# First mixture: last rows stored from spare buffers, node numbers read as rows and turned by PE; results of both mixtures read back by SP and POOL, two mask rows by POOL

## The chip, the cores and the metric

The kernel runs on one core of a Trainium2 chip. Its time is the device time of one execution in microseconds. Three runs of the kernel before gave a median of 2898.42 us (2892.7 to 2900.67). The engines are called PE (matmul, with its weight loads as PEld), DVE (vector), ACT (scalar), POOL (GpSimd) and SP (which here only issues transfers). ACT, POOL and SP each issue DMA transfers from their own queue of instructions.

## What is computed

A graph of 2708 nodes with 256 features passes through four layers. Each layer adds a graph attention and then a second network to x:

```
x = x + gnn_i(layernorm(x), adj) ;  x = x + ffn_i(layernorm(x))      i = 0..3
ffn_0: slice attention with a scan      ffn_1: first mixture (top 1 of 8)
ffn_2: attention, then second mixture   ffn_3: one linear layer
       (top 2 of 8, SwiGLU)
ffn_1: H = gelu(x W1 + b1)                     2708 x 1024
       p = softmax(H Wg + bg);  e = argmax(p)  one of 8 experts for each node
       y = (H Wd[e] + bd[e]) * p[e]            2708 x 256
```

gnn_1 is an attention over the neighbours in four heads, gnn_2 and gnn_3 have one head.

## The kernel before, in words

All is float32. The nodes are 22 tiles of 128 rows, the last of 20; x lies in SBUF as `X`. A tiling framework keeps each engine's instructions in program order (but for those put behind a named one by `issue_after`), sets the semaphores, and hands out buffers from pools: a tile with `bufs=3` waits for what used the one three before it. A pool's tiles of one tag share the same buffers.

**First mixture** (`top1_ffn`). The first loop goes over six blocks of 512 nodes (four tiles; the last has two). For each: `hidden` (PE L911, gelu on ACT L915) makes H transposed, in two halves of four 128-wide slices; `features` normalizes and turns the next block; `gate` makes the logits; `Routing.chunk` counts each node's place among those of its expert, and POOL scatters the node's number, 4 bytes, to that place of a list in DRAM `fnodes` (L1444, a tile an instruction). `store` turns H back to rows: for each tile and half four PE transposes (L926), a copy from PSUM into `hr` (L927, on DVE for the first half and on ACT for the second), and a store of 128 x 512 numbers by SP (L930) into DRAM `hidden`. `hr` has three buffers, which `q4` of the gate shares. Blocks 0 to 3 are stored in their own turn; blocks 4 and 5, six tiles and twelve stores, only after the gate of block 5.

Then `finish` computes how the list is cut into tiles of 128 places: a first tile for each of the eight experts, and further tiles up to 26 (`usual`); what lies beyond is run under a condition (`others`). SP loads the node numbers: `load_first` those of the first eight tiles (L1554, 128 partitions with eight numbers each), `load` one further tile at a time (L1550, one number to a partition), each with a start that SP reads from a register. `numbers` (L980) casts them to integers; `places` computes where the results go. For each tile: `fetch` (L990, POOL) gathers 128 rows of `hidden`, `transposes` (L1003, copies L1004) turns them, L1035 multiplies by the expert's `wd`, L1041 adds `bd`, and `send` (L1573, POOL) scatters the results to DRAM. Numbers and places of later tiles are made in groups of four, two tiles ahead of the first gather that needs them (`s + 6 == g[0]`, where four are fetched ahead). `owners` and `weights` (with the softmax over the logits, copied at L1532) stand behind the first cast; ACT's part of the next layer's preparation is `Head`.

**Reading the results back** (`combine`, for both mixtures, one choice in the first and two in the second). Six blocks are read with 128 x 4 x 256 numbers, 512 KB, each (the last as 128 and 20 rows); the issuing engine alternates (L1594). DVE adds each tile into X with its weight (L1604). All reads are issued ahead of the adds. The next graph layer follows at once: statistics of the rows (L144, L145), a square root on ACT (L147, which needs a table load after other functions), reciprocal (L151), normalized rows (L108), PE transposes (L1134).

**Mask.** The attention loops multiply by a mask (L675 and its like) in 22 row tiles. `mark_empty` writes two rows for nodes without neighbours into its last tile (L2053, L2054, from `flags`), once ahead of the loop of the second layer (near 691 us) and once in `reload_graph`, where the mask is read again after the second mixture has used its room: a memset by POOL (L2058), 22 loads by SP (L2060) and the two rows by ACT.

In the built program the transfers of SP and ACT take eight completion semaphores in turn, and those of POOL eight others; a transfer waits for the one eight before it in that row.

Of the kernel before, what the change touches and what calls it, by code (L numbers as in the profile page):

```python
# [16 lines left out]
P = 128  # L17
# [839 lines left out]
def top1_ffn(net, ctx):  # L857
# [6 lines left out]
    with ExitStack() as inner:  # L864
# [21 lines left out]
        with tc.tile_pool(name="f1tp", bufs=2, space=PSUM) as ptp, tc.tile_pool(  # L886
            name="f1h", bufs=2, space=PSUM
        ) as ph, tc.tile_pool(name="f1g", bufs=1, space=PSUM) as pg, tc.tile_pool(
            name="f1r", bufs=2
        ) as rp, tc.tile_pool(name="f1work", bufs=2) as work:  # L890
            w1 = work.tile([P, 2, HID], F32, name="w1", bufs=1)
            nc.gpsimd.dma_start(w1, a["f1_w1"].rearrange("(c p) m -> p c m", p=P))

            def features(its):
                ft = work.tile([P, 2, 512], F32, name="ft")
                for k, t in enumerate(its):
                    r = rows(t)
                    f = rp.tile([P, D], F32, name="f", bufs=2)
                    net.normed(f, t, ln)
                    ps = net.transposed(ptp, f, r)  # L900
                    nc.vector.tensor_copy(ft[:, :, k * P : k * P + r], ps[:, :, :r])
                return ft

            def hidden(ft, nw):

                wide, bufs = (512, 3) if nw == 512 else (nw, 2)
                halves = [work.tile([P, KC // 2, wide], F32, name=f"ht{wide}", bufs=bufs) for _ in range(2)]
                for k in range(KC):
                    ps = ph.tile([P, 512], F32, name="h")
                    for c in range(2):  # L910
                        nc.tensor.matmul(  # L911
                            ps[:, :nw], w1[:, c, k * P : (k + 1) * P], ft[:, c, :nw], start=c == 0, stop=c == 1
                        )
                    part = halves[k // (KC // 2)][:, k % (KC // 2), :]
                    nc.scalar.activation(part[:, :nw], ps[:, :nw], AF.Gelu, bias=b1[:, k : k + 1])  # L915
                return halves

            def store(its, halves):

                for k, t in enumerate(its):  # L920
                    r = rows(t)
                    for n, half in enumerate(halves):
                        hr = rp.tile([P, 512], F32, name="hr", bufs=3)
                        ps = pg.tile([P, 4, P], F32, name=f"hr{n}")
                        for c in range(KC // 2):
                            nc.tensor.transpose(ps[:r, c, :], half[:, c, k * P : k * P + r], net.ident)  # L926
                        (nc.scalar.copy if n else nc.vector.tensor_copy)(  # L927
                            hr[:r], ps[:r].rearrange("p c m -> p (c m)")
                        )
                        nc.sync.dma_start(rows_of[span(t), n * 512 : (n + 1) * 512], hr[:r])  # L930

            def gate(its, halves, nw):
                ht = [half[:, k, :] for half in halves for k in range(KC // 2)]
                pq = pg.tile([P, 512], F32, name="pq")
                for c in range(KC):
                    g = c % 4 * 32
                    nc.tensor.matmul(pq[g : g + 32, :nw], wg[:, c, :], ht[c][:, :nw], start=c < 4, stop=c >= 4)
                q4 = rp.tile([P, 512], F32, name="q4", tag="hr", bufs=3)
                nc.vector.tensor_copy(q4[:, :nw], pq[:, :nw])
                pr = pg.tile([P, 4, E], F32, name="pr")  # L940
                for k, t in enumerate(its):
                    r = rows(t)
                    nc.tensor.matmul(pr[:r, k, :], q4[:, k * P : k * P + r], add4, start=True, stop=True)
                    nc.vector.tensor_tensor(route.logits[:r, t, :], pr[:r, k, :], bg[:r], ALU.add)
                for _ in route.chunk(rp, pg, its[0], len(its), None):
                    pass


            blocks, kept = chunks(512), []
            ft = features(tiles_of(*blocks[0]))  # L950
            for n, (n0, nw) in enumerate(blocks):
                its = tiles_of(n0, nw)
                halves = hidden(ft, nw)
                if n + 1 < len(blocks):
                    ft = features(tiles_of(*blocks[n + 1]))
                gate(its, halves, nw)
                kept.append((its, halves))
                if n + 2 != len(blocks):
                    for k in kept:
                        store(*k)  # L960
                    kept.clear()
        route.finish()
        prep = ctx.enter_context(tc.tile_pool(name="g2prep", bufs=1))
        with tc.tile_pool(name="f1t", bufs=1, space=PSUM) as pt, tc.tile_pool(
# [2 lines left out]
            bd = sp.tile([P, E, D], F32, name="bd", bufs=1)  # L967
            nc.scalar.dma_start(bd.rearrange("p e d -> p (e d)"), a["f1_bd"].rearrange("e d -> (e d)").partition_broadcast(P))

            node, number, to = (  # L970
                sp.tile([P, route.tiles], t, name=name, bufs=1)
                for t, name in ((F32, "node"), (I32, "number"), (I32, "to"))
            )
            usual = route.usual
            groups = [range(E)] + [range(s, min(s + 4, usual)) for s in range(E, usual, 4)]
            held = {}

            def numbers(group):
                g = slice(group[0], group[-1] + 1)
                nc.vector.tensor_copy(number[:, g], node[:, g])  # L980

            def places(group):
                g = slice(group[0], group[-1] + 1)
                at = sp.tile([P, E], F32, name="at", bufs=2)[:, : len(group)]
                nc.vector.tensor_tensor(at, node[:, g], route.taken[:, g], ALU.mult)
                nc.vector.tensor_tensor(to[:, g], at, route.spare[:, g], ALU.add)

            def fetch(s):
# [21 lines left out]
                    return slice(s, s + 1)  # L1010
                return bass.ds(engine.value_load(route.expert[0:1, s : s + 1], min_val=0, max_val=E - 1), 1)

            route.load_first(node[:, :E])
            for s in range(E, usual):
                route.load(s, node[:, s : s + 1])
            numbers(groups[0])
            for s in range(4):
                fetch(s)
            ready = transposes(0)
            route.owners()  # L1020
            places(groups[0])
            route.weights(one)
            heads = []

            def through(s0, s1, ready):
                last = added = None
                for s in range(s0, s1):
# [13 lines left out]
                    added = nc.vector.tensor_tensor(y, ps, bd[:, e, :].rearrange("p e d -> p (e d)"), ALU.add)  # L1041
                    route.send(to[:, s : s + 1], y)
                    with tc.issue_after(added.ins):
                        for g in groups[1:]:
                            if s + 6 == g[0]:
                                numbers(g)
                                places(g)
                        if s == 3:
                            heads.append(Head(net, prep, one, "g2", True, nc.scalar))
                    if s + 4 < s1:  # L1050
# [2 lines left out]
            through(0, usual, ready)  # L1053
            with route.others():
                group = range(usual, route.tiles)
                for s in group:
                    route.load(s, node[:, s : s + 1])
                numbers(group)
                places(group)
                for s in group:  # L1060
                    fetch(s)
                through(usual, route.tiles, transposes(usual))
# [259 lines left out]
class Routing:  # L1322
# [216 lines left out]
    def load(self, s, f):  # L1539

        sync = self.net.nc.sync
        if s < self.E:
            self.loaded = sync.dma_start(f, self.hs[s * CAP : s * CAP + P, :])
            return

        with nullcontext() if s == self.usual else self.net.tc.issue_after(self.loaded.ins):
            row = sync.value_load(
                self.row[0:1, s : s + 1], min_val=0, max_val=(self.E - 1) * CAP + (NT - 1) * P
            )
        self.loaded = sync.dma_start(f, self.hs[bass.ds(row, P), :])  # L1550

    def load_first(self, f):

        self.loaded = self.net.nc.sync.dma_start(  # L1554
            f, self.hs.rearrange("(e c) d -> c (e d)", e=self.E)[:P, :]
        )

    def where(self, work, s, f):
# [24 lines left out]
    def combine(self, pool):  # L1583
# [3 lines left out]
        for n, (n0, nw) in enumerate(chunks(512)):  # L1587
            its = tiles_of(n0, nw)
            ys = []
            for c in range(self.choices):  # L1590
                y = pool.tile([P, 4, D], F32, name=f"y{c}", bufs=len(chunks(512)))
                for k0, k1, r in whole_and_rest(its):
                    r0 = (c * NT + its[k0]) * P
                    (nc.sync, nc.scalar)[(n + c) % 2].dma_start(  # L1594
                        y[:r, k0:k1, :],
                        self.ys[r0 : r0 + (k1 - k0 - 1) * P + r, :].rearrange("(t p) d -> p t d", p=r),
                    )
                ys.append(y)
# [450 lines left out]
def mark_empty(net):  # L2049

    row = net.mask[SPARE : SPARE + 1, LAST, :]
    whole = LAST * P
    net.nc.scalar.dma_start(row[:, :whole], net.flags[:LAST])  # L2053
    net.nc.scalar.dma_start(row[:, whole:], net.flags[LAST:NT, : N - whole])  # L2054


def reload_graph(net, kept):
# [101 lines left out]
```

## Time and profile before

| what | value |
|---|---|
| median of three runs (lowest to highest) | 2898.42 us (2892.7 to 2900.67) |
| the profiled execution's own time | 2896.45 us |
| its span, first to last instruction | 2894.7 us |
| granted PE clock, mean over the span | 0.946 |
| PE, PEld busy | 2651.2 us (92%), 1624.4 us (56%) |
| DVE, ACT, POOL busy | 1441.4 (50%), 1041.2 (36%), 369.5 us (13%) |
| instructions | 32765 |
| DMA | 113729 packets, 197.70 MB |

The profile is one execution. "Busy" leaves out waits and the issuing of transfers. In the lists of the trace, a row in order of time has the start, the duration, the engine and the program's line, the operation with what it writes and reads, and in brackets how long the engine had been idle and what released it; `SPq`, `ACTq` and `POOLq` are the issues of transfers by these engines. A releaser is inferred: where several were awaited, the last by the records is named. The first mixture's last stores lie near 1211 to 1234 us, the read-back of the first mixture near 1366 to 1394 us, that of the second near 2577 to 2600 us.

### The profile page before, as it was taken

How to read it: one execution, taken by the hardware profiler on the slowest of the kernel's cores; microseconds unless marked ns; L12 is line 12 of the kernel's file. 1: busy time of each engine (PE TensorE's matmuls, PEld its weight loads, DVE VectorE, ACT ScalarE, POOL GpSimd, SP SyncE). 2: the span in 40 equal slices, each digit the busy share in tenths (PEclk: the TensorE clock that was granted, in tenths of full speed). 3: DMA queues.
4: the chain of work that ended last, by engine and by line, in shares of the span. 5: the costliest groups of instructions: out<-in, count | busy, mean ns of one | idle time of the engine just before them, and what ended most of it. 6: DMA issues, size and time to landing. Idle time of an engine off the chain costs nothing. (4 is left out here: it accounts for less than half of the span.)

```text
span 2894.7 us, 32765 instructions
## 1 busy us (share of the span) xinstructions
PE 2651.2 (92%) x11893; PEld 1624.4 (56%) x11893; DVE 1441.4 (50%) x3062; ACT 1041.2 (36%) x1658; POOL 369.5 (13%) x462
## 2 busy tenths in 40 slices
PE   6999989799999989878899899998979999969998
PEld 5667746563333334567688433333346677747885
DVE  7753358344777774432644455455543222235455
ACT  3344433224665643211543223233312222215453
POOL 0000012100000001133300123223321111110002
PEclk9999999698999998989999999899969999989999
DMA  8899210000000005354200100002021111041001
GB/s 298 280 292 312 104 65 1 8 1 1 1 1 1 1 19 173 91 166 130 87 1 0 34 22 17 15 0 93 15 101 41 34 30 34 28 137 59 1 1 39
DMA packets 113729, 197.70 MB, mean 68 GB/s; under 512 B 12380, under 2 KB 71636, under 8 KB 110732
## 3 DMA queue, kind: packets, MB, share of 16 engines
q1 hardware_dynamic: 92758, 147.89, 16.1%
q0 software_dynamic: 13120, 38.06, 4.0%
q10 hardware_dynamic: 7690, 9.62, 1.1%
q8 instruction: 99, 1.62, 0.2%
q14 instruction: 62, 0.51, 0.1%
HBM read 135.82 MB, written 59.71 MB: 68 GB/s over the span
## 5 line engine op out<-in xcount | busy, mean ns | idle before, releaser
L675 DVE SCALAR_TENSOR_TENSOR e<-e,mask 128x768 f32<-128x768 f32 (+2 forms) x264 | 411.7, 1574 | 310.9 <-ACT e L674 310.7
L674 ACT ACTIVATE e<-big_p,minus_one,ratio 128x768 f32<-128x768 f32 (+2 forms) x264 | 394.9, 1513 | 363.4 <-PE acc L1236 229.8
L1236 PE MATMUL acc<-V,e 128*128 128x257 f32 (+1 forms) x1936 | 433.5, 383 | 4.5 <-DVE e L675 4.4
L1236 PEld LDWEIGHTS acc<-V,e 128*128 128x128 f32 (+1 forms) x1936 | 352.3, 186 | 85.7 <-issue 32.1
L780 PE MATMUL acc<-e,V 128*64 128x512 f32 (+1 forms) x1056 | 249.7, 550 | 4.1 <-DVE e L675 4.1
L1878 PE MATMUL h<-w,ft 128*128 (+1 forms) x752 | 233.0, 452 | 0.5 <-ACT ft L1860 0.5
L284 PE MATMUL acc<-F,e 128*128 128x257 f32 x968 | 226.3, 384 | 3.3 <-DVE e L281 2.9
L284 PEld LDWEIGHTS acc<-F,e 128*128 128x128 f32 x968 | 173.4, 185 | 67.3 <-DVE e L281 28.7
L780 PEld LDWEIGHTS acc<-e,V 128*64 128x64 f32 x1056 | 95.4, 137 | 180.6 <-issue 159.0
L1719 PE MATMUL sc<-qt,kt 64*128 64x512 f32 (+4 forms) x656 | 187.0, 535 | 4.1 <-ACT e L1729 2.4
L1729 ACT ACTIVATE e<-sc 128x1024 f32<-128x1024 f32 (+4 forms) x140 | 102.8, 760 | 204.5 <-PE sc L1719 188.4
L1878 PEld LDWEIGHTS h<-w,ft 128*128 128x128 f32 x752 | 136.0, 191 | 56.7 <-issue 1.4
L281 DVE TENSOR_TENSOR e<-e,mask 128x512 f32<-128x512 f32 (+2 forms) x132 | 80.4, 625 | 149.4 <-ACT e L275 147.8
L1737 DVE TENSOR_TENSOR sum<-sum,e 128x1024 f32<-128x1024 f32 (+4 forms) x102 | 103.8, 1018 | 99.1 <-ACT e L1729 97.4
L275 ACT ACTIVATE e<-score 128x512 f32<-128x512 f32 (+2 forms) x132 | 69.7, 544 | 179.2 <-PE score L273 153.0
L1734 PE MATMUL po<-e,V 128*64 128x512 f32 (+5 forms) x560 | 119.4, 511 | 14.8 <-ACT e L1729 8.8
L1910 PE MATMUL po<-w,ht 114*128 (+1 forms) x564 | 129.5, 379 | 0.9 <-DVE ht L1903 0.9
L1719 PEld LDWEIGHTS sc<-qt,kt 64*128 64x128 f32 x656 | 71.8, 198 | 94.8 <-issue 80.9
L788 PE MATMUL den<-e,low 128*3 128x512 f32 (+1 forms) x1056 | 123.1, 542 | 0.0
L1910 PEld LDWEIGHTS po<-w,ht 114*128 114x128 f32 x564 | 106.7, 189 | 22.6 <-DVE ht L1903 8.2
L1563 DVE TENSOR_SCALAR second<-f,down 128x1 f32<-128x1 f32 x47 | 10.0, 213 | 213.6 <-DMA f<-hs 213.6
L273 PE MATMUL score<-QK 128*128 128x512 f32 (+2 forms) x264 | 112.1, 554 | 1.2 <-ACT e L275 0.7
(605 smaller groups left out, 3501.0 us busy)
## 6 DMA issues: line engine op xcount, KB each, us to landing
row<-in_adj SPq DMA_DIRECT2D x21, 1354.0 KB
raw<-in_adjT SPq DMA_DIRECT2D x35, 768.0 KB
hs<-zero SPq DMA_DIRECT2D x8, 2838.0 KB
hidden<-hr SPq DMA_DIRECT2D x42, 256.0 KB
wd<-in_f_wd SPq DMA_DIRECT2D x8, 1024.0 KB
kept<-mask SPq DMA_DIRECT2D x21, 338.5 KB
mask<-kept SPq DMA_DIRECT2D x21, 338.5 KB
f<-hs SPq DMA_DIRECT2D x47, 129.0 KB
```

The source lines that it names most:

```text
L273: nc.tensor.matmul(ps[:r, :iw], QK[:, 0, span(j)], QK[:, 1, i0 : i0 + iw], start=True, stop=True)
L284: nc.tensor.matmul(acc[k][:ri], e[:r, k * P : k * P + ri], F[:r, j, :], start=j == 0, stop=j == NT - 1)
L674: nc.scalar.activation(v, big_p[:, i], AF.Relu, bias=net.minus_one, scale=ratio)
L675: return nc.vector.scalar_tensor_tensor(v, v, 1.0, net.mask[:, j, i], ALU.add, ALU.mult)
L780: nc.tensor.matmul(acc[n][half, :iw], V[:, j, h, :], e[:, k, i0 : i0 + iw], start=j == 0, stop=j == NT - 1)
L788: nc.tensor.matmul(den[g : g + Q, :iw], low[:, j, h, Q - 1 - q : 2 * Q - 1 - q], e[:, k, i0 : i0 + iw], start=False, stop=j == NT - 1 and ...
L1236: nc.tensor.matmul(acc[k][:ri], e[:, k * P : k * P + ri], V[:, j, :], start=j == 0, stop=j == NT - 1)
L1719: nc.tensor.matmul(ps[:r, g, o:iw], kt[b, span(j)], qt[b, o:iw], start=True, stop=True)
L1734: nc.tensor.matmul(po[b, o:iw], V[:r, j, g, :], e[:r, g, o:iw], start=j == 0, stop=j == last)
L1737: (nc.gpsimd if part else nc.vector).tensor_tensor(total, total, e[:r, :, o:iw], ALU.add)
L1878: last = nc.tensor.matmul(halves[s, n][:, q, :HALF], fts[s][:, c, :], weights.w13[n][:, es[s], c, q * HALF : (q + 1) * HALF], start=c == 0 ...
L1910: last = nc.tensor.matmul(po, ht[:KP, k, :], w2[:KP, es[s], k, :], start=k == 0, stop=k == KC - 1)
```

## The change

The twelve stores of blocks 4 and 5 move behind the loop. All their copies are made by ACT. The eight copies of block 4 go into eight slices of three tiles of the loop's own pool (two with the tag of `ft`, one with the tag of `ht512`), the four of block 5 into the three `hr` buffers. The node numbers are loaded as rows: a tile's 128 numbers lie in one partition of `rowed`, the first eight tiles in partitions 0 to 7, the next nine from partition 32 and the last nine from partition 64. `numbers` turns a group by a PE transpose into PSUM and casts from there; `places` reads the same PSUM tile. So there are three groups instead of six (8, 9 and 9 tiles in place of 8, 4, 4, 4, 4 and 2). In both mixtures the read-back alternates between SP and POOL instead of SP and ACT, and the two mask rows are issued by POOL instead of ACT, at both places.

```diff
@@ -915,16 +915,18 @@
                     nc.scalar.activation(part[:, :nw], ps[:, :nw], AF.Gelu, bias=b1[:, k : k + 1])
                 return halves
 
-            def store(its, halves):
-
+            def store(its, halves, late=False, room=()):
+
+
+                room = list(room)
                 for k, t in enumerate(its):
                     r = rows(t)
                     for n, half in enumerate(halves):
-                        hr = rp.tile([P, 512], F32, name="hr", bufs=3)
+                        hr = room.pop(0) if room else rp.tile([P, 512], F32, name="hr", bufs=3)
                         ps = pg.tile([P, 4, P], F32, name=f"hr{n}")
                         for c in range(KC // 2):
                             nc.tensor.transpose(ps[:r, c, :], half[:, c, k * P : k * P + r], net.ident)
-                        (nc.scalar.copy if n else nc.vector.tensor_copy)(
+                        (nc.scalar.copy if n or late else nc.vector.tensor_copy)(
                             hr[:r], ps[:r].rearrange("p c m -> p (c m)")
                         )
                         nc.sync.dma_start(rows_of[span(t), n * 512 : (n + 1) * 512], hr[:r])
@@ -955,10 +957,15 @@
                     ft = features(tiles_of(*blocks[n + 1]))
                 gate(its, halves, nw)
                 kept.append((its, halves))
-                if n + 2 != len(blocks):
-                    for k in kept:
-                        store(*k)
-                    kept.clear()
+                if n + 2 < len(blocks):
+                    store(*kept.pop())
+
+            spare = [work.tile([P, 2, 512], F32, name="spare", tag="ft") for _ in range(2)]
+            spare.append(work.tile([P, KC // 2, 512], F32, name="spare", tag="ht512", bufs=3))
+            room = [t[:, k, :] for t in spare for k in range(t.shape[1])]
+            for k in kept:
+                store(*k, True, room)
+                room = ()
         route.finish()
         prep = ctx.enter_context(tc.tile_pool(name="g2prep", bufs=1))
         with tc.tile_pool(name="f1t", bufs=1, space=PSUM) as pt, tc.tile_pool(
@@ -967,22 +974,32 @@
             bd = sp.tile([P, E, D], F32, name="bd", bufs=1)
             nc.scalar.dma_start(bd.rearrange("p e d -> p (e d)"), a["f1_bd"].rearrange("e d -> (e d)").partition_broadcast(P))
 
-            node, number, to = (
-                sp.tile([P, route.tiles], t, name=name, bufs=1)
-                for t, name in ((F32, "node"), (I32, "number"), (I32, "to"))
-            )
+            number, to = (sp.tile([P, route.tiles], I32, name=name, bufs=1) for name in ("number", "to"))
             usual = route.usual
-            groups = [range(E)] + [range(s, min(s + 4, usual)) for s in range(E, usual, 4)]
+            groups = [range(E)] + [range(s, min(s + 9, usual)) for s in range(E, usual, 9)]
+            rowed = sp.tile([P, P], F32, name="rowed", bufs=1)
             held = {}
 
-            def numbers(group):
+            def load(group, at):
+                node = rowed[at : at + len(group), :]
+                if group[0] == 0:
+                    route.load_first(node)
+                else:
+                    for k, s in enumerate(group):
+                        route.load(s, node[k : k + 1, :])
+
+            def numbers(group, at):
                 g = slice(group[0], group[-1] + 1)
-                nc.vector.tensor_copy(number[:, g], node[:, g])
-
-            def places(group):
+                here = slice(at, at + len(group))
+                ps = pt.tile([P, len(group)], F32, name="node", bufs=1)
+                nc.tensor.transpose(ps, rowed[here, :], net.ident[here, here])
+                nc.vector.tensor_copy(number[:, g], ps)
+                return ps
+
+            def places(group, ps):
                 g = slice(group[0], group[-1] + 1)
-                at = sp.tile([P, E], F32, name="at", bufs=2)[:, : len(group)]
-                nc.vector.tensor_tensor(at, node[:, g], route.taken[:, g], ALU.mult)
+                at = sp.tile([P, E + 1], F32, name="at", bufs=1)[:, : len(group)]
+                nc.vector.tensor_tensor(at, ps, route.taken[:, g], ALU.mult)
                 nc.vector.tensor_tensor(to[:, g], at, route.spare[:, g], ALU.add)
 
             def fetch(s):
@@ -1010,15 +1027,14 @@
                     return slice(s, s + 1)
                 return bass.ds(engine.value_load(route.expert[0:1, s : s + 1], min_val=0, max_val=E - 1), 1)
 
-            route.load_first(node[:, :E])
-            for s in range(E, usual):
-                route.load(s, node[:, s : s + 1])
-            numbers(groups[0])
+            for n, g in enumerate(groups):
+                load(g, 32 * n)
+            first = numbers(groups[0], 0)
             for s in range(4):
                 fetch(s)
             ready = transposes(0)
             route.owners()
-            places(groups[0])
+            places(groups[0], first)
             route.weights(one)
             heads = []
 
@@ -1041,10 +1057,9 @@
                     added = nc.vector.tensor_tensor(y, ps, bd[:, e, :].rearrange("p e d -> p (e d)"), ALU.add)
                     route.send(to[:, s : s + 1], y)
                     with tc.issue_after(added.ins):
-                        for g in groups[1:]:
+                        for n, g in enumerate(groups):
                             if s + 6 == g[0]:
-                                numbers(g)
-                                places(g)
+                                places(g, numbers(g, 32 * n))
                         if s == 3:
                             heads.append(Head(net, prep, one, "g2", True, nc.scalar))
                     if s + 4 < s1:
@@ -1053,10 +1068,8 @@
             through(0, usual, ready)
             with route.others():
                 group = range(usual, route.tiles)
-                for s in group:
-                    route.load(s, node[:, s : s + 1])
-                numbers(group)
-                places(group)
+                load(group, 0)
+                places(group, numbers(group, 0))
                 for s in group:
                     fetch(s)
                 through(usual, route.tiles, transposes(usual))
@@ -1547,12 +1560,13 @@
             row = sync.value_load(
                 self.row[0:1, s : s + 1], min_val=0, max_val=(self.E - 1) * CAP + (NT - 1) * P
             )
-        self.loaded = sync.dma_start(f, self.hs[bass.ds(row, P), :])
+        rows_of = self.hs[bass.ds(row, P), :]
+        self.loaded = sync.dma_start(f, rows_of.rearrange("p d -> d p") if self.choices == 1 else rows_of)
 
     def load_first(self, f):
 
         self.loaded = self.net.nc.sync.dma_start(
-            f, self.hs.rearrange("(e c) d -> c (e d)", e=self.E)[:P, :]
+            f, self.hs.rearrange("(e c) d -> e (c d)", e=self.E)[:, :P]
         )
 
     def where(self, work, s, f):
@@ -1591,7 +1605,7 @@
                 y = pool.tile([P, 4, D], F32, name=f"y{c}", bufs=len(chunks(512)))
                 for k0, k1, r in whole_and_rest(its):
                     r0 = (c * NT + its[k0]) * P
-                    (nc.sync, nc.scalar)[(n + c) % 2].dma_start(
+                    (nc.sync, nc.gpsimd)[(n + c) % 2].dma_start(
                         y[:r, k0:k1, :],
                         self.ys[r0 : r0 + (k1 - k0 - 1) * P + r, :].rearrange("(t p) d -> p t d", p=r),
                     )
@@ -2050,8 +2064,8 @@
 
     row = net.mask[SPARE : SPARE + 1, LAST, :]
     whole = LAST * P
-    net.nc.scalar.dma_start(row[:, :whole], net.flags[:LAST])
-    net.nc.scalar.dma_start(row[:, whole:], net.flags[LAST:NT, : N - whole])
+    net.nc.gpsimd.dma_start(row[:, :whole], net.flags[:LAST])
+    net.nc.gpsimd.dma_start(row[:, whole:], net.flags[LAST:NT, : N - whole])
 
 
 def reload_graph(net, kept):
```

## The prediction

> **What bounds the kernel now.** I read the page's chain first, then waits and timeline of the stages that the change touches, then stretches of busy time. The chain:
>
> ```profile
> PE 18%; DMA 3%; DVE 2%; issue 1%; ACT 0%; POOL 0%; ACTq 0%; DVEq 0%; POOLq 0%
> ```
>
> Its shares sum to about 24%: it reaches back only to 2166 us, so it says nothing of the first mixture. PE is busy 92% of the span, so what this change can win lies in PE's gaps. The waits between 1205 and 1256 us (total, times, longest) show the first gap:
>
> ```profile
> POOL hr L990 <- DMA node<-fnodes: 23.0, 1, 23.0
> PE ht L1003 <- DMA node<-fnodes: 17.1, 1, 17.1
> ACT hr L927 <- DMA hidden<-hr: 11.4, 3, 7.8
> DVE hr L927 <- DMA hidden<-hr: 7.6, 2, 4.0
> ```
>
> The copies into hr wait for earlier stores from the same three buffers; then POOL's gather and PE wait for the node numbers. In order of time (start, duration):
>
> ```profile
> 1231.23 0.57 ACT L927 COPY hr<-hr 20x512 f32<-20x512 f32 x1 [2.15 <-DVE fspare L1519]
> ...
> 1234.23 0.41 SPq L1554 DMA_DIRECT2D node<-fnodes  x1
> ...
> 1241.48 0.17 DVE L980 CAST number<-node 128x8 int32<-128x8 f32 x1 [6.20 <-DMA node<-fnodes]
> ...
> 1242.54 1.00 POOL L990 DMA_INDIRECT hr<-hidden,number  x1 [23.00 <-DMA node<-fnodes]
> ...
> 1251.88 4.62 PE L1035 MATMUL y<-wd,ht 128*128 128x256 f32 x16
> ```
>
> Last copy, its store, number load, cast, gather, transposes, first product: one chain, with nothing beside it. From 1251.88 to 1364.31 PE is busy 111.97 of 112.43 us, at 4.33 us a tile: there nothing is to be won, and what comes earlier at its head comes earlier at its end. Why the stores land late, by stretches (PE, PEld, DVE, ACT, POOL, clock, DMA share, GB/s):
>
> ```profile
> 1184.00:1195.00 11.00, 11.00 (x53) 6.79 (x52) 5.88 (x26) 4.52 (x8) 2.30 (x3) 1.00 0.52 191
> 1218.00:1225.00 7.00, 2.44 (x9) 1.43 (x8) 2.45 (x11) 0.26 (x1) 1.23 (x2) 0.50 0.94 74
> ```
>
> Storing one block of rows moves 191 GB/s at a share of 0.52; behind the last six scatters of node numbers (L1444, issued 1212.3 to 1218.65) the engines are full at 74 GB/s. The second gap is in the last graph layer, where the second mixture's results are read back:
>
> ```profile
> 2576.82 12.74 ACTq L1594 DMA_DIRECT2D y<-dys  x7
> ...
> 2582.18 3.26 DVE L1604 SCALAR_TENSOR_TENSOR X<-y,dweight,X 128x256 f32<-128x256 f32 x8 [5.52 <-DMA y<-dys]
> ...
> 2587.10 3.23 DVE L1604 SCALAR_TENSOR_TENSOR X<-y,dweight,X 128x256 f32<-128x256 f32 x8
> ...
> 2594.28 0.76 ACTq L2054 DMA_DIRECT2D mask<-flags  x1
> 2595.07 1.28 ACT L147 ACT_TABLE_LOAD   x1 [21.37 <-DMA y<-dys]
> 2596.36 0.30 ACT L147 ACTIVATE sd<-mv,ln_eps 128x4 f32<-128x4 f32 x1
> 2596.69 0.18 DVE L151 RECIPROCAL rstd<-sd 128x4 f32<-128x4 f32 x1 [6.37 <-ACT sd L147]
> 2596.91 1.38 DVE L108 TENSOR_SCALAR f<-X,mv,rstd 128x256 f32<-128x256 f32 x4
> ...
> 2597.47 1.73 PE L1134 MATMUL tp<-ident,f 128*128 128x128 f32 x7 [24.18 <-DVE f L108]
> ```
>
> ACT stands in its queue until seven reads and two mask rows are issued; DVE, done with block 1 at 2590.33, waits 6.37 us for a square root, and PE idles 24.2 us.
>
> **Part by part.**
>
> *Last stores.* Before, twelve copies alternate between DVE and ACT over three buffers, from 1211.03 to 1231.8. After, ACT makes all twelve, 0.59 us each; a pair costs transposes of about 0.6 and a copy of 0.59 with gaps of 0.15 on each of two PSUM tiles, some 1.6 us a pair, so eight copies into spare buffers end near 1218 and none waits for a store. But the twelfth still goes into the ring and waits for the ninth copy's store to land. Ten stores of 256 KB and two of 40 KB are 2.64 MB. At the clear rate (191 GB/s over a share of 0.52, 367 GB/s) the first nine, 2.36 MB, need 6.4 us from 1212.3; the scatters add what they cost in the stretch 1218 to 1225 and just ahead of it: 7.0 us at a share of 0.94 for 0.52 MB that would take 1.4, so 5.2, and (1215 to 1218: 0.34 MB at 113 GB/s, share 0.53) another 0.7; with a microsecond until the first bytes move the ninth lands near 1226 to 1227. Copy 0.6, hop 0.1, issue to landing 2.4 (the last store before: 1231.83 to 1234.2): the number load starts near 1230.0, 4.2 us earlier. Bounds: the last scatter lands at 1228.1, and the load waits for it too, so at most 6.1 earlier; all stores crawling at 74 GB/s puts the ninth at 1218 + (2.36 - 0.79 - 0.34)/0.074, 1234.6, and the load at 1237.9, 3.7 later. I take **-4.2**, nearest to the stretch measured with the same bytes and scatters. What it frees on DVE (six copies of 0.69) is hidden behind these stores, and the softmax over the logits, which now waits for the eighth store, is through by 1231.5, ahead of the numbers; if it were late, its 4.2 us would stand on the path.
>
> *Numbers as rows.* The load takes 1234.23 to 1241.48, 7.25 us, for 1024 numbers of 4 bytes; after, eight rows of 512 bytes. The 20-row stores give 2.4 for issue and landing; added are one PE transpose (0.4 by the 20-row L926 ones at the idle clock, 385 to 421 ns) and a hop of 0.15; the cast of 0.17 stays, and POOL's 0.89 behind it. 7.25 - 2.4 - 0.55 is **-4.3** (bounds -5 and, if a row landed like the 40 KB behind traffic, -2). The 18 single loads keep their 1.09 us pitch on SP; nine are there by 1242, before the second group is asked for at the third tile. Their two transposes and casts stand between PE's tiles: **+0.4** in all; `bd`, 1 MB and more from ACT, is issued with the number load and was through (241 GB/s to 1241) before the first gather; now the gather meets its tail: **+1.0** (0 to 2). This head: -4.2 - 4.3 + 1.0 + 0.4 = **-7.1**.
>
> *Results by SP and POOL, second mixture.* SP keeps seven reads, POOL takes seven; ACT has none, so its table is loaded near 2575 and the square root follows the statistics (2587.18), ready while DVE adds block 1. DVE's reciprocal then comes at 2590.4 instead of 2596.69: **-6.3**. Next late is DVE itself. The price is on POOL: its direct transfers take 0.5 to 0.9 us to issue and start later, so block 0 comes late by **+0.9** (one issue and a wait; bounds 0 and 4.5, the row wx<-in_w_x of 512 KB that landed in 9.8 against 5.4 here). The bytes are the same and run at 313 GB/s either way; blocks then come every 2.9 us and DVE takes 6.4 a block. Behind POOL's reads are only the mask's memset (2.35) and the two mask rows, whose tile is the last of 22 in the loop at L675, begun at 2638.8 with some 1.25 us a tile: wanted near 2665, some 70 us later. SP's 22 mask loads start earlier, behind SP's own reads; they ended at 2616, and that loop starts at 2638. Sum **-5.4** (0 to -6.3).
>
> The Trainium skill ("DMA: Bandwidth & Descriptors", Issuing engines are not separate DMA queues) says that issuing from several engines saves only the sequencer's issue time, usually small. By it ACT would win its seven issues alone, 3.9 us by their durations, and the sum would be 2.4 us higher; the row of 21.37 us of ACT idle speaks for more. The same page (SWDGE vs HWDGE vs iDMA) sends plain copies to SP and ACT and gives first bytes after 1 us from POOL against 0.6; with that 0.4 in place of 0.9 the sum would be 0.5 lower.
>
> *First mixture's read-back.* ACT's four issues and table load end at 1371.1 and it is not asked before 1376.02: nothing on the path. SP's first read has less beside it while POOL prepares; DVE waited 4.44 us for it: **-0.5** (-1 to +2, if POOL's block 1, wanted at 1375.9, lands after 9.8).
>
> *Mask rows by POOL, near 691.* ACT's two issues (0.87 and 0.76) lay between its last four exponentials, which PE's products waited for: **-0.6** (0 to -1.6); POOL is idle there.
>
> Sum: -7.1 - 5.4 - 0.5 - 0.6 = **-13.6**, so 2896.45 becomes 2882.9. The profiled execution (span 2894.7) lies 2.0 under the median of 2898.42; half of that is added here and below, so **2884**.
>
> **Rivals.**
> - *Stores crawl.* All of them queue beside the scatters at 74 GB/s: the load is 3.7 later, the head +3.7 - 4.3 + 1.4 = +0.8, the sum -5.7: 2892. For it: the stretch above. Against: in it only three stores were open at a time and the engines were full with single numbers.
> - *Stores end with the scatters:* the load at 1228.1, head -9.0, and block 0 on time (-6.3): sum -16.4, 2881.
> - *ACT's gap passes to DVE*, which waits 9.8 us for POOL's block 0, as wx landed: second gap -1.9, first mixture +2, sum -7.6, 2890.
> - *POOL's reads go one at a time* (the slower side). If a 512 KB read takes 9.8 us and the next begins only then, the second mixture's fifth lands at 2625.9 and the two small ones some 6 later; the adds end near 2633.9 instead of 2621.2, +12.7; in the first mixture block 3 comes at 1387.7 instead of 1385.5, +2.2. With -7.1 - 0.6: +7.2, 2905. It decides from a pitch of about 8.6 us. Against it: POOL's gathers of 512 KB, issued 1.3 us apart, land 1.4 to 2.8 apart.
>
> **Chances.** Forecast 0.52 (2876 to 2888), stores with the scatters 0.16, stores crawl 0.15, POOL late 0.08, one at a time 0.09. A measurement of this kernel tells about 0.3%, 8.7 us, from no change: 2889.7 to 2907.1. Faster by more: 0.52 + 0.16 and a little of POOL late, 0.70; within: the crawl, the rest of POOL late and a little of the last, 0.22; slower, if the pitch is near 10 us or more: 0.08. The range reaches from the second rival, less the low ends of the gather (1.0), the numbers (0.7) and the mask rows (1.0) and some 3 for the spread of the runs, to the first rival with 2 of that spread: 2875 to 2894.
>
> **What would show it.** The number load (L1568 after) near 1230.0 relative to the same block, and 2.4 us until PE's transpose; the first product near 1244.5; the copies into spare waiting for no store, the twelfth waiting for the ninth. In the second gap the table load near 2575 and PE at about 2592 instead of 2597.5. Wrong would be: stores under 100 GB/s past 1230, POOL's reads landing over 8 us apart, DVE waiting on y in blocks 1 to 5, or a gap of DVE for the logits' softmax.

## The result, and the profile after

The changed kernel takes 2881.09 us (median of 9 runs, 2871.93 to 2886.57), the kernel before 2896.05 us (9 runs, 2889.15 to 2900.67). The ratio is 0.9946, with a 95% interval of 0.9934 to 0.9959: 15.6 us less (11.9 to 19.1). The profiled execution of the changed kernel took 2884.97 us (span 2883.3 us), 11.5 us less than that of before.

The chain that ended last reaches the whole span this time, and is mostly PE:

```profile
PE 76%; DVE 9%; DMA 5%; issue 4%; ACT 3%; POOL 2%; ACTq 0%; POOLq 0%; SPq 0%; DVEq 0%
```

The waits of the first mixture's head in the changed kernel, 1202 to 1246 us (total, times, longest):

```profile
POOL hr L1007 <- DMA bd<-in_f_bd: 15.5, 1, 15.5
...
PE node L995 <- DMA rowed<-fnodes: 14.9, 1, 14.9
ACT hr L929 <- DMA hidden<-hr: 9.2, 1, 9.2
```

Twelve copies now have one wait for a store, the twelfth's. POOL's releaser is named `bd` because it came last by the records; its gather follows the cast. The same stage in order of time:

```profile
1224.68 0.57 ACT L929 COPY hr<-hr 20x512 f32<-20x512 f32 x1 [9.21 <-DMA hidden<-hr]
...
1227.30 0.28 SPq L1568 DMA_DIRECT2D rowed<-fnodes  x1
...
1230.27 0.24 PE L995 MATMUL node<-ident,rowed 8*128 8x8 f32 x1 [14.93 <-DMA rowed<-fnodes]
1230.55 0.17 DVE L996 CAST number<-node 128x8 int32<-128x8 f32 x1 [1.82 <-PE node L995]
...
1231.52 1.00 POOL L1007 DMA_INDIRECT hr<-hidden,number  x1 [15.51 <-DMA bd<-in_f_bd]
...
1239.80 3.62 PE L1051 MATMUL y<-wd,ht 128*128 128x256 f32 x16
```

From the number load to the first gather it is 4.22 us instead of 8.31. The stretches (busy us of PE, PEld, DVE, ACT, POOL, then clock, DMA share, GB/s) show that the stores now run beside the scatters: the DMA engines are full until 1222 us, at 154 GB/s.

```profile
1207.00:1215.00 8.00, 7.34 (x63) 5.69 (x58) 6.50 (x39) 5.63 (x11) 4.83 (x5) 1.00 0.79 190
1215.00:1222.00 7.00, 0.34 (x4) 0.06 (x1) 1.92 (x12) 0.47 (x1) 0.90 (x1) 0.80 1.02 154
1222.00:1228.00 6.00, 0.00 (x0) 0.00 (x0) 1.90 (x6) 2.21 (x3) 0.00 (x0) 0.50 0.46 62
```

The second gap, in order of time. The table is loaded before the reads begin, the square root follows the statistics at once, and PE waits 18.62 us instead of 24.18. New is a wait of DVE inside block 0, for POOL's first read (2.46 us).

```profile
2568.70 1.28 ACT L147 ACT_TABLE_LOAD   x1 [0.90 <-ACTq L1538]
...
2570.64 10.32 SPq L1608 DMA_DIRECT2D y<-dys  x7
...
2571.09 4.92 POOL L1608 DMA_DIRECT2D y<-dys  x7 [0.46 <-issue]
2574.64 0.88 DVE L1618 SCALAR_TENSOR_TENSOR X<-y,dweight,X 128x256 f32<-128x256 f32 x2 [3.93 <-DMA y<-dys]
...
2577.98 2.46 DVE L1618 SCALAR_TENSOR_TENSOR X<-y,dweight,X 128x256 f32<-128x256 f32 x6 [2.46 <-DMA y<-dys]
...
2582.23 0.30 ACT L147 ACTIVATE sd<-mv,ln_eps 128x4 f32<-128x4 f32 x1 [12.25 <-DVE mv L145]
...
2586.02 1.73 PE L1147 MATMUL tp<-ident,f 128*128 128x128 f32 x7 [18.62 <-DVE f L108]
```

### The profile page after: what moved, and what is told of

It reads as the page before. It is cut to its first block, busy times and chain, and to the rows that moved or that the text cites. A ratio compares the mean times of both kernels' runs of the same rounds, so it can differ in the third digit from the quotient of the medians.

```text
span 2883.3 us, 32755 instructions
## 1 busy us (share of the span) xinstructions
PE 2649.7 (92%) x11896; PEld 1624.0 (56%) x11896; DVE 1437.2 (50%) x3047; ACT 1044.3 (36%) x1664; POOL 378.6 (13%) x477
## 3 DMA queue, kind: packets, MB, share of 16 engines
q1 hardware_dynamic: 89178, 147.89, 15.6%
## 4 chain that ended last, share of the span: by engine, by line
PE 76%; DVE 9%; DMA 5%; issue 4%; ACT 3%; POOL 2%; ACTq 0%; POOLq 0%; SPq 0%; DVEq 0%
PE acc L1249 15%; PE acc L780 8%; PE acc L284 7%; PE den L788 4%; PE po L1924 4%; PE po L1748 4%; PE sc L1733 4%; PE score L273 3%; PE h L1892 3%; PE pv L123 3%; PE h L911 3%; DMA f<-hs 2%; PE po L123 2%; PE sc L1711 2%; PE pl L123 1%
```

## The experiments

Whole times scatter by some 10 us from run to run, so each part is read in its own stage of the trace. All figures are us. Landings are read from the trace's records of the completion semaphores, which a transfer raises when it is through. "Load" counts from the last product of block 5's gate (L937, its last record; the first expectation below counts from that group's first record, 1.12 earlier) to the number load; "gather" from there to the first gather; "product" from there to the first L1035; "gap 1" and "gap 2" are PE's idle time ahead of L1134 in the two read-backs; "mask" runs from the last product into `pv` near 688 to the first into `acc`.

| kernel | load | gather | product | gap 1 | gap 2 | mask | median, ratio to before (95%) |
|---|---|---|---|---|---|---|---|
| before | 24.17 | 8.31 | 9.33 | 14.43 | 24.18 | 9.24 | |
| changed | 20.45 | 4.22 | 8.28 | 14.32 | 18.62 | 8.52 | 2881.09, 0.9946 (0.9934 to 0.9959) |
| stores alone | 22.44 | 7.81 | 9.31 | 14.10 | 23.94 | 9.20 | 2900.18, 1.0 (0.9985 to 1.0015) |
| rows alone | 23.52 | 3.44 | 9.24 | 14.45 | 24.13 | 9.29 | 2895.27, 0.998 (0.9961 to 0.9999) |
| SP and POOL reads alone | 23.62 | 7.84 | 8.71 | 14.59 | 18.63 | 9.16 | 2892.95, 0.9983 (0.9968 to 0.9998) |
| mask rows alone | 24.16 | 7.51 | 9.06 | 13.94 | 18.54 | 8.49 | 2884.17, 0.9953 (0.9938 to 0.9969) |
| SP reads alone | 23.84 | 8.31 | 9.69 | 13.41 | 16.36 | 9.17 | 2885.94, 0.9957 (0.994 to 0.9974) |
| changed, room for 12 | 23.00 | 3.51 | 9.11 | 14.86 | 18.59 | 8.44 | 2882.39, 0.9943 (0.9925 to 0.9962) |
| changed, room for the twelfth | 20.33 | 3.88 | 11.06 | 14.52 | 18.69 | 8.59 | 2878.85, 0.9946 (0.9926 to 0.9966) |
| changed, first rows only | 19.75 | 3.67 | 10.72 | 14.62 | 18.59 | 8.48 | 2883.37, 0.994 (0.9918 to 0.9962) |
| changed, SP reads | 21.07 | 3.75 | 8.20 | 13.03 | 16.34 | 8.55 | 2877.58, 0.9927 (0.99 to 0.9954) |
| changed, by block | 20.88 | 3.75 | 8.25 | 14.21 | 16.34 | 8.54 | 2881.95, 0.9939 (0.9916 to 0.9962) |
| room for the twelfth, SP reads | 20.11 | 3.97 | 11.41 | 13.18 | 16.47 | 8.47 | 2880.0, 0.9941 (0.992 to 0.9962) |

**One part of the change at a time.** The first four are the kernel before with one piece of the diff each.

*Stores alone* (`store` with `late` and `room`, the calls behind the loop):

> The kernel before with its last stores alone changed: behind the loop, copies on ACT, eight into spare buffers. Theory (the parts of the first mixture's head add up, and the stores are worth what the number load gained, 21.57 us after the last gate product instead of 25.29): number load 3.7 us earlier, nothing else, first product 3.7 us earlier, time -3.7 us. Rival (the stores gain only together with the rows, since single numbers take longer behind them): number load 3.7 us earlier but landing longer than 7.25 us, first product less than 2 us earlier.

The load came 1.7 earlier, not 3.7, and the first product 2.3. Neither theory: the numbers landed no later (7.81). The trace shows ACT standing twice between its copies, released by nothing that the profile knows, while stores and scatters filled the DMA engines:

```profile
1216.69 0.59 ACT L929 COPY spare<-hr 128x512 f32<-128x512 f32 x1 [2.56 <-remote]
...
1219.57 0.58 ACT L929 COPY spare<-hr 128x512 f32<-128x512 f32 x1 [2.29 <-remote]
```

So the ninth copy, whose store the twelfth awaits, came some 4 us late. The trace says a little more than "remote": both copies waited on the semaphore that PE raises, which rose at 1216.67 and 1219.55, though PE's transposes for them are recorded as ended by 1214.35 and 1214.84. Why it rose so late stays open.

*Rows alone* (`rowed`, PE transposes, groups of nine, both loads as rows):

> The kernel before with the node numbers alone changed: rows, PE transpose, groups of 8, 9 and 9. Theory: from the number load to the first gather 4.2 us instead of 8.3 (-4.1), from the gather to the first product 8.3 instead of 9.3 (-1.0, since 18 loads of 128 single numbers no longer run beside the gathers), the later transposes +0.3: time -4.8 us. Rival (the gather was quicker for the earlier bd, which the stores moved no more than the load): gather to product stays 9.3 us, time -3.8 us.

The time from the load to the gather fell by 4.87, more than expected; the product time hardly moved (9.24), as the rival on the gathers had it. Why is taken up below.

*SP and POOL reads alone*, and *mask rows alone*:

```diff
-                    (nc.sync, nc.scalar)[(n + c) % 2].dma_start(
+                    (nc.sync, nc.gpsimd)[(n + c) % 2].dma_start(
```

> The kernel before with the reads alone changed, SP and POOL instead of SP and ACT; the mask rows stay on ACT. Theory (ACT's reads, not its two mask rows, hold up the square root): second gap of PE 18.6 us instead of 24.2, first mixture's read-back -0.5, time -6. Rival (ACT's mask rows alone do it, as they wait for landings ahead of the table load): ACT issues them late and the second gap stays over 22 us, time -0.5 to -2.

```diff
-    net.nc.scalar.dma_start(row[:, :whole], net.flags[:LAST])
-    net.nc.scalar.dma_start(row[:, whole:], net.flags[LAST:NT, : N - whole])
+    net.nc.gpsimd.dma_start(row[:, :whole], net.flags[:LAST])
+    net.nc.gpsimd.dma_start(row[:, whole:], net.flags[LAST:NT, : N - whole])
```

> The kernel before with the mask rows alone on POOL, at both places; ACT keeps its reads. First theory (ACT's reads hold up the square root): second gap shortened by the two rows' own issue, some 1.6 us, and 1.3 near 691 us, time -2.9. Rival (the rows wait for landings from 2589.6 to 2595.0, and without them the table load follows the last read): second gap 19.1 us instead of 24.2, with 1.3 near 691 us time -6.4; then reads and rows do not add up, since either move alone frees ACT.

Each alone brings gap 2 to 18.6: the theory on the reads and the rival on the rows are both right, and the two do not add. With the reads still on ACT, the table load follows the last of them (issued 2579.43) directly, and DVE waits 0.99 instead of 6.37:

```profile
2580.00 1.28 ACT L147 ACT_TABLE_LOAD   x1 [15.73 <-DVE X L1604]
2581.29 0.30 ACT L147 ACTIVATE sd<-mv,ln_eps 128x4 f32<-128x4 f32 x1
2581.62 0.18 DVE L151 RECIPROCAL rstd<-sd 128x4 f32<-128x4 f32 x1 [0.99 <-ACT sd L147]
...
2582.39 1.73 PE L1134 MATMUL tp<-ident,f 128*128 128x128 f32 x7 [18.54 <-DVE f L108]
```

In the kernel before ACT's last read went out at 2589.01, and from there to the table load at 2595.07 only the two rows stood in its queue:

```profile
2592.17 0.82 ACTq L2053 DMA_DIRECT2D mask<-flags  x1
2594.28 0.76 ACTq L2054 DMA_DIRECT2D mask<-flags  x1
2595.07 1.28 ACT L147 ACT_TABLE_LOAD   x1 [21.37 <-DMA y<-dys]
```

With the reads moved and the rows left, the second row is late as well, but behind the square root; it holds ACT's next copy, and PE loses 2.58 after the gap:

```profile
2585.51 0.76 ACTq L2054 DMA_DIRECT2D mask<-flags  x1
2586.32 0.38 ACT L1140 ACTIVATE ft<-tp 128x256 f32<-128x256 f32 x1 [7.49 <-DMA mask<-kept]
...
2586.85 4.39 PE L123 MATMUL pv<-g3w,ft 128*128 128x257 f32 x12 [2.58 <-ACT ft L1140]
```

Over the whole run the mask rows alone gained 13.6 us (9.0 to 18.0), twice the 6.4 of their two stages (5.6 and 0.75). No stage that they touch holds the rest. At equal mean granted clock, 0.947, two of these runs took 2888.85 and 2889.51 us and three of the kernel before 2894.43 to 2895.88, a difference of 4.9 to 7.0; so the rest seems to go with the clock, which the last section comes back to. Whether the edit itself raised the clock is not shown.

**Who reads.** The changed kernel with all reads by SP (`nc.sync.dma_start(`), then with `(nc.sync, nc.gpsimd)[n % 2]`, so that block 0 comes from SP alone:

> The changed kernel with every read of results issued by SP, none by POOL. Theory (what counts is that ACT is free; the bytes move at 313 GB/s whoever issues them): second gap within 1 us of 18.6, time within 1 us of the changed kernel. Rival (one engine's reads go one after another, or its completion semaphores hold them): blocks of 1 MB come over 6.4 us apart, DVE waits for y in later blocks, and time is 5 us or more above the changed kernel.

> The changed kernel with both choices of a block read by one engine, SP for blocks 0, 2 and 4, POOL for 1, 3 and 5 (no change in the first mixture). Theory (DVE's wait of 2.46 us in block 0 is for POOL's first read): that wait shrinks to under 1 us, second gap 1.5 to 2 us shorter, time -1.5 to -2 against the changed kernel. Rival (the wait is for bandwidth, as both reads move at once): the wait stays above 2 us and the gap within 0.5 us.

Both shorten gap 2 to 16.34, 2.3 less, where the theory for SP alone had expected no change. DVE's wait was for POOL's read of block 0: in the changed kernel it landed 7.25 us after the first read's issue, and DVE went on at 7.34. SP alone also shortens gap 1, to 13.03. Alone, SP's reads did land one after another, but only 1.5 us apart (the ten of 512 KB), so that block 0 was complete after 5.54 and block 1 was there when DVE wanted it. The last of the fourteen landed after 18.74 us with SP alone and after 18.70 with SP and POOL. So POOL's part in the reads is a cost: by the landings the second half of block 0 came third, behind a read of block 1 by SP, and the third read with SP alone landed at 7.04. What counts is that ACT is free. The same edit made to the kernel before, mask rows left on ACT:

> The kernel before with all reads of results issued by SP and nothing else; the mask rows stay on ACT. Theory (either move frees ACT, and POOL's reads are no gain but a later block 0): second gap 16.3 us instead of 24.2 and the first read-back's gap 13.0 instead of 14.4, time -9.2. Rival (SP alone is quick only because POOL takes the mask rows): ACT's mask rows wait behind the reads for completion semaphores that SP and ACT share, the table load comes after 2590 us, and the second gap stays above 20 us.

Gap 2 is 16.36, gap 1 13.41. The rows now go out early, as ACT has no reads ahead of them (the first follows POOL's memset, which ended at 2577.41), and the table is there in time:

```profile
2574.56 13.12 SPq L1594 DMA_DIRECT2D y<-dys  x14
...
2577.43 1.31 ACTq L2053 DMA_DIRECT2D mask<-flags  x1
...
2578.78 0.76 ACTq L2054 DMA_DIRECT2D mask<-flags  x1
2579.57 1.28 ACT L147 ACT_TABLE_LOAD   x1 [7.96 <-DMA y<-dys]
```

The Trainium skill ("DMA: Bandwidth & Descriptors", Issuing engines are not separate DMA queues) says that transfers from any engine interleave on the same DMA engines, so that a second issuer saves only issue time. The runs agree: all fourteen reads had landed 18.7 us after the first issue with SP alone and with SP and POOL, 19.0 us with SP and ACT.

**What bounds the number load.** The changed kernel with a buffer for every late copy, then with one more buffer, for the twelfth alone:

```diff
-            for k in kept:
+            last = work.tile([P, 2, HID], F32, name="spare", tag="w1", bufs=1)
+            rooms = [room, [last[:, k // 2, k % 2 * 512 : (k % 2 + 1) * 512] for k in range(4)]]
+            for k, room in zip(kept, rooms):
                 store(*k, True, room)
-                room = ()
```

> The changed kernel with room for all twelve late halves (the last four in the room of w1), so that the twelfth copy waits for no store. Theory (after this wait the last scatter, landing 16.4 us after its block's last scatter could start, is next): number load at the landing of the last scatter, 1.6 to 1.8 us earlier than in the changed kernel, time -1.7 against it. Rival (the DMA engines are full until then and the last stores only queue longer): last store lands as late as before, number load less than 0.5 us earlier.

The load came 2.6 later. In the built order a transfer of the next layer's weights stood on ACT ahead of the last two copies, and with it the copies waited for the scatters to land, at 1227.10:

```profile
1227.47 0.38 ACTq L1088 DMA_DIRECT2D g2w<-in_g_w  x1
1227.89 0.57 ACT L929 COPY spare<-hr 20x512 f32<-20x512 f32 x1 [11.91 <-DMA fnodes<-ftag,fto]
```

> The changed kernel with one further buffer, in the room of w1, for the twelfth copy, so that it waits for no landed store, and with ACT's transfers of the next layer behind all twelve copies (with room for all twelve they stood ahead of the last two and held them until the scatters landed). Theory (the last scatter's landing is the next limit, 18.6 to 19.6 us after the last product of the gate): number load 19 us after that product instead of 20.5 to 21.1, time -1.5 against the changed kernel. Rival (the twelve stores end as late however early they are issued): number load at 20.5 or later, time the same; then what bounds is the bytes beside the scatters.

```diff
-                        hr = room.pop(0) if room else rp.tile(...)
+                        hr = room.pop(0) if room else last if late and n and r < P else rp.tile(...)
...
+            last = work.tile([P, 512], F32, name="spare", tag="w1", bufs=1)
```

The twelfth store was issued at 1220.97, 13.71 after the gate's last product instead of 18.43, and the load still stood at 20.33, nearer to the rival's 20.5 than to the theory's 19. The issues of SP, and SP's waits from 1218 to 1229 (total, times, longest), show what it waited for:

```profile
1220.97 0.29 SPq L932 DMA_DIRECT2D hidden<-spare  x1
...
1227.59 0.32 SPq L1569 DMA_DIRECT2D rowed<-fnodes  x1
```

```profile
SPq L1569 <- DMA hidden<-spare: 3.6, 1, 3.6
...
SPq L1569 <- DMA hidden<-hr: 0.8, 2, 0.5
```

It was the stores and not the scatters. The last scatter landed at 1225.82, 18.6 after the gate's last product; the last five stores landed from 1226.02 to 1227.32, and the load went out 0.27 after the last of them. So the twelfth store, issued 4.7 earlier than in the changed kernel, landed at 20.06 instead of 20.25. The trial does not settle what the load would do without the ring's wait, though: ACT again stood still twice (2.33 and 0.92), and the eighth to eleventh stores went out 3.2 to 4.2 later than in the changed kernel, where the eleventh landed at 18.5, with the scatters. Where the load stands ahead of the twelfth store (first rows only, below), it went out 0.13 after the last scatter landed, at 19.62: there the scatters are the limit.

*Both edits together:*

> The last kernel with all reads of results issued by SP. Theory (the two are in different stages and add up): second gap of PE 16.3 us and first read-back's 13.0 us as with SP alone, number load as in the kernel with the further buffer; together -3.6 and -1.5 against the changed kernel, some 20.7 us under the kernel before. Rival (the number load is bound by the bytes): -3.6 against the changed kernel alone.

The reads kept their gain (gaps 13.18 and 16.47); the load did not follow the theory's 19: the further buffer brought it 0.3 to 1.0 forward (20.11 against 20.45 and 21.07) and lost 3.2 on the product. ACT stood still twice here too (1.75 and 2.98). Of all versions the changed kernel with SP's reads has the best stages, 3.6 (1.29 + 2.28) below the changed kernel by its gaps, and the lowest ratio, 0.9927; its interval (0.99 to 0.9954) overlaps that of the changed kernel.

**The first gathers.** Rows for the first eight tiles only; the other 18 as 128 single numbers each:

> The changed kernel with rows for the first eight tiles alone; the other 18 are loaded as 128 single numbers again, without a transpose. Theory (these loads slow the first gathers): gather to first product 9.3 us instead of 8.3, the two later transposes gone (-0.3): time +0.7 against the changed kernel. Rival (the gathers were quicker for another reason): 8.3 us stays, time -0.3.

Product 10.72: neither. The first product stands behind the second tile's transposes in PE's order, so it follows the second gather. What orders the kernels with rows is when `bd` landed, counted from the issue of the first gather: 0.5 to 0.8 after it, and the product came at 8.20 to 8.28 (changed, SP reads, by block); 1.2 to 1.4 after, 9.11 and 9.24 (room for 12, rows alone); 4.2 and 4.4 after, 11.06 and 11.41 (the two with a buffer for the twelfth, where another load, `av`, was issued 0.7 to 1.05 behind the first gather as well). With single numbers and `bd` landed 2.6 to 3.0 ahead it came at 8.71 to 9.69; with single numbers and `bd` landed 2.5 after, at 10.72. So `bd`'s tail does slow the gathers, and the single numbers seem to cost about as much as the 1.2 to 1.4 of the second group. This is an order found afterwards; no run moved `bd` or the single numbers by itself.

## Why the prediction was right

The time lies 2.9 us under the 2884 forecast, and the sum holds by stages. The time alone would fit the rival "stores end with the scatters" (2881) as well; the stages rule that one out, as the load went out 1.9 after the last scatter's landing and block 0 came late. Step by step, means over kernels that have and have not the edit in that stage:

- *Last stores, -4.2:* -3.1 (load 23.86 in the five kernels without, 20.80 in changed, SP reads and by block). The ninth store let the twelfth copy go 17.8 after the gate's last product, where I had about 16.4. The rival "stores crawl" is out. My bound of 6.1 took the last scatter's landing from before (18.1 after the gate's last product); in the kernels with the late stores it landed at 18.3 to 19.6. Twelve stores are 2.70 MB and not 2.64, which enters nothing else.
- *Numbers as rows, -4.3:* -4.2 (7.96 with single numbers, 3.77 with rows). Right.
- *The gather meets bd's tail, +1.0:* it does, as `bd` landed 0.5 after the first gather's issue, but the time to the product fell by 1.0 (9.20 in the four kernels with neither stores nor rows, 8.24 in changed, SP reads and by block). What my sum left out is the other side: the 18 loads of single numbers no longer run beside the gathers. That this is the reason is argued from the order above and not shown by a run. Where `bd` landed later the tail cost 0.9 and more. *The later transposes, +0.4:* nothing seen (111.97 us of products before, 111.58 after).
- *Second mixture's read-back, -5.4:* -5.5. The size was right, the reason half right. I had ACT stand in its queue for seven reads and two rows and gave the gain to the reads; the two rows alone, waiting 5 us behind the last read, were enough. My price of POOL's later block 0 (+0.9) was 1.2: DVE's adds of that block ended 9.8 after the first read's issue, where they ended 8.6 after it in the kernel before; against SP alone (7.4) the price is 2.4. A block of 1.05 MB at 313 GB/s comes every 3.35 us and not every 2.9, which changes nothing, as DVE takes 6.4.
- *First mixture's read-back, -0.5:* +0.3 (14.23 without, 14.52 with POOL's reads); SP alone would have given -1.0. Mis-signed and small.
- *Mask rows near 691, -0.6:* -0.7 (9.21 to 8.51). Right.

Sum -3.1 - 4.2 - 1.0 - 5.5 + 0.3 - 0.7 = -14.2 where I had -13.6, against 15.6 (11.9 to 19.1) measured. That the two sums are so close is partly luck: the stores (by 1.1) and the first read-back (by 0.8) gave less than I took, the gathers (by 2.0) and the later transposes (by 0.4) more. "POOL's reads go one at a time" is out by its price: they did land in order, but 1.9 to 2.1 us apart and not 8.6 or more. "ACT's gap passes to DVE" is out too, as DVE went on after 7.34 us and not 9.8.

The parts were not additive in two places. Reads and rows, tried alone, gain 5.5 and 5.6 in gap 2, and together 5.6. In the head stores and rows alone give 1.6 and 4.9 of the 8.2 (from the gate's last product to the first product, 41.15 without, 39.56, 36.20, and 32.9 with both); the rest, 1.7, would be ACT's standstill in the one run (its load is 1.6 above 20.80) and `bd`'s later landing in the other (its product is 1.0 above 8.24), which is inferred from these two stages.

## What to carry to other kernels

Before a transfer is moved from one queue to another, read what stands between the last useful issue and the instruction that is late: here two small rows behind ACT's seven reads held the square root, and moving either the rows or the reads was enough. And try the plainest queue first: with one engine that has nothing else to do the first block was there 1.7 us sooner than with two, and the last at the same time. A wait removed from a ring of buffers is worth only what the next limit leaves: here the load moved by 0.1 to 1.0 us, as other stores, issued late, landed late in its stead, and the first product lost 2.8 to 3.2.

## What was not expected of the hardware

The stage from the first scores (L1719) to the second mixture's first product (L1878), which no edit touches, took 499.7 to 515.0 us in these profiles, with a mean granted clock of 0.94 to 0.90. It is 4.4 us longer in the changed kernel's profile than in that of before. That is one reason why the profiled executions differ by 11.5 only, while the stages that the edits touch are together 15.3 shorter (8.9 from the gate's last product to the first product, 5.6 and 0.1 in the gaps, 0.7 at the mask). One place shows how. PE idles 2.35 us in both; then in the kernel before the clock is back after one stretch of 4 us (the sixth number behind the stretch is the clock):

```profile
2073.60:2075.90 2.30, 0.00 (x0) 0.00 (x0) 0.00 (x0) 0.00 (x0) 2.26 (x2) 1.00 0.20 70
2075.90:2079.90 4.00, 3.97 (x16) 2.04 (x16) 2.49 (x1) 0.00 (x0) 0.00 (x0) 0.58 0.00 0
2079.90:2083.90 4.00, 3.50 (x26) 2.06 (x25) 2.71 (x5) 1.46 (x4) 0.00 (x0) 1.00 0.00 0
```

In the changed kernel it stays at half for some 17 us, with PE as busy:

```profile
2059.20:2061.50 2.30, 0.00 (x1) 0.00 (x0) 0.00 (x0) 0.00 (x0) 2.28 (x2) 1.00 0.21 74
2061.50:2065.50 4.00, 3.94 (x16) 2.08 (x16) 2.61 (x1) 0.12 (x1) 0.01 (x1) 0.60 0.00 0
2065.50:2069.50 4.00, 3.86 (x20) 2.14 (x19) 1.74 (x4) 1.22 (x4) 0.00 (x0) 0.50 0.00 0
...
2073.50:2077.50 4.00, 4.00 (x14) 2.44 (x14) 0.85 (x2) 1.71 (x6) 2.27 (x3) 0.50 0.00 0
2077.50:2081.50 4.00, 4.00 (x26) 2.31 (x25) 1.36 (x3) 1.37 (x5) 1.21 (x2) 0.77 0.00 0
```

Single profiles cannot tell whether the change made this likelier; the spread within the changed kernel's own nine runs is 14.6 us, and it goes with the mean clock (0.954 to 0.955 in the four shortest, 0.948 to 0.951 in the other five). The Trainium skill ("TensorE: Matmul & The Clock Gate", The HAM clock gate) says that the clock is judged over free-running windows of about 3.4 us and that one busy window restores it. The first case agrees: the trace has the clock at half for 3.41 us. The second, 17.07 us or five such stretches with PE busy, does not.
